# Fused sequence kernel, attention stage: which engine copies the first turned block and evicts q

## Chip, cores and metric

The kernel runs on one core of one Trainium2 chip. A core has a matrix engine (TensorE, PE in the profile, with PEld for its weight loads), a vector engine (VectorE, DVE), a scalar engine (ScalarE, ACT), a general one (GpSimd, POOL), a sync engine whose queue issues most DMAs here (SyncE, SP), and DMA engines. Each engine works through its own queue in order; semaphores tie them together. The metric is the device time of the whole program in microseconds (us), lower is better; the median over runs counts.

## The reference, cut to what matters

Four layers follow each other over 8 batches of 512 x 512 numbers: a grid step (finite differences of `f` with coefficient grids), an attention block with a feed-forward network, a mixture-of-experts feed-forward, and a low-rank gated response. The change is in the attention:

```python
q = (x @ Wq + bq).reshape(B, S, N_HEAD, HEAD_DIM).transpose(0, 2, 1, 3)
k = (x @ Wk + bk).reshape(B, S, N_HEAD, HEAD_DIM).transpose(0, 2, 1, 3)
v = (x @ Wv + bv).reshape(B, S, N_HEAD, HEAD_DIM).transpose(0, 2, 1, 3)
scores = jnp.einsum('bhqd,bhkd->bhqk', q / math.sqrt(HEAD_DIM), k)
scores = scores + attention_bias
scores = jnp.where(src_mask, -jnp.inf, scores.astype(jnp.float32))
probs = jax.nn.softmax(scores, axis=-1).astype(v.dtype)
ctx = jnp.einsum('bhqk,bhkd->bhqd', probs, v)
```

There are 16 heads of 32 features; everything is computed in 32-bit floats.

## The kernel before

**Stages.** `fused_kernel` runs a grid stage for batch 0, then `attention_stage` over all 8 batches, then `mlp_stage`. The attention stage also does the grid step of the next batches on the side: `grid_step` deals out the operations in the table `GRID`, mostly on VectorE (`gv`, line 697, and line 798), with a ReLU (line 804) and a small DMA issue behind it (line 806) on ScalarE, for each half of a batch's rows.

**Steps.** The main loop (from line 1137) goes over 128 units `(b, c, r)`: batch, group of four heads, quarter of the 512 query rows. A step of the loop has three units in hand. For the one of two steps ago TensorE multiplies probabilities with v (`values`, every second step). For the one of the step before, `turned` transposes the probabilities on TensorE (line 570, into tiles `tr` of PSUM) and copies them to SBUF (`pt`, lines 1052 and 1054). For the present one `softmax` adds the bias and takes the row's extreme on VectorE (line 1022, `mn`), and exponentiates on ScalarE (line 1027). The step ends with `scores` of the next unit. Between them, in `fill`, lie the projections: `q_block`, `k_block`, `v_block` and `o_block` (TensorE, line 567), the way of the next batch's x into transposed form (`x1_in`) and back (`x1_back`), and the loads of its mask (`load_mask`: a DMA, line 588, and a conversion on ScalarE, line 593). GpSimd adds the mask to the bias (line 998). In the texts below, step t of batch b is the pass of the loop in which the present unit is number t = 4c + r of that batch; it turns unit t - 1.

**What sets the order.** Nearly every instruction is pinned by `keep_in_program_order`, so each engine's queue is the order of the Python code. In `turned` the four heads of a unit come in two calls, u = 0 with heads 0 and 1, u = 1 with heads 2 and 3. There are two `tr` tiles, so the transposes of head 2 need head 0 copied out, those of head 3 need head 1. A rule (lines 1046 to 1054) says which engine copies: head 1 and head 3 always ScalarE, head 2 always VectorE, and head 0 by a list `early` of units, VectorE where it isn't in the list. The list is all of the first 8 units in batch 0, (1, 3, 4, 5, 7, 9, 15) in batches 1 to 6, and empty in batch 7.

**q.** `q_block` (line 634) multiplies into one PSUM tile of tag `m`, which the other projections and `add_bv` (the row `pb`) share, and VectorE writes it to SBUF with the bias added and scaled by 1/sqrt(32) (line 643). k's eviction (line 663) is on ScalarE.

**The bias of q** comes by a DMA (line 181) into `bqk[:, 0, :]`, 128 partitions of 4 numbers.

Of the kernel before, what the change touches and what calls it, by code (L numbers as in the profile page):

```python
# [15 lines left out]
AF = mybir.ActivationFunctionType  # L16
ALU = mybir.AluOpType
# [15 lines left out]
QSCALE = 1.0 / math.sqrt(HD)  # L33
# [6 lines left out]
def fused_kernel(ctx: ExitStack, tc: tile.TileContext, a: dict):  # L40
# [155 lines left out]
    def load_late():  # L196
# [3 lines left out]
    wl3 = const.tile([P, KC, RK], F32, name="wl3")  # L200
    x1d = [dram.tile([P, R, D], F32, name=f"x1d_{b}") for b in range(NB)]
    first = attention_stage(
        tc, a, small, dram, xp, xt, x_home, x1d, grid, ident, sc1, shift, io, wo8, w, (bqk, bvc, bo),
        g2, mhalf, load_w, load_late,
# [340 lines left out]
def attention_stage(  # L545
# [12 lines left out]
    nc = tc.nc  # L558
    with ExitStack() as ctx:
# [4 lines left out]
        pin = tc.keep_in_program_order  # L564
# [4 lines left out]
        def tp(out, src):  # L569
            pin(nc.tensor.transpose(out, src, ident))  # L570


        bqk, bvc, bo = rows
# [53 lines left out]
        def block(out, lhsT, rhs):  # L627

            def half(h):
                for k in (2 * h, 2 * h + 1):  # L630
                    mm(out, lhsT(k), rhs(k), k == 0, k == KC - 1)
            return half

        def q_block(b, c, tag="m"):
            pr = ps.tile([P, S], F32, name=f"pq_{b}_{c}", tag=tag)
            half = block(
                pr, lambda k: w["Wq"][:, k, c * P : (c + 1) * P], lambda k: x1s[b, k]
            )
            yield half(0)
            yield half(1)  # L640
            t = pp.tile([P, S], F32, name=f"qt_{b}_{c}", tag="qt")
            pin(
                nc.vector.tensor_scalar(
                    t.rearrange("f (r p) -> f r p", r=R), pr.rearrange("f (p r) -> f r p", r=R),
                    bqk[:, 0, c : c + 1], QSCALE, ALU.add, ALU.mult,
                )
            )
            qs[b, c] = t
# [266 lines left out]
        def halves(b):  # L915

            for g in (
                q_block(b, 1), k_block(b, 1), q_block(b, 2), k_block(b, 2), o_block(b - 1, 0),
                q_block(b, 3), k_block(b, 3), *(o_block(b - 1, r) for r in (1, 2, 3)),
            ):  # L920
                next(g)
                yield
                for _ in g:
                    pass
                yield

        def fill(b, t):
# [15 lines left out]
            if n == NB:  # L943
                if t == 0:
                    head["fill"] = halves(b)
                jobs.append(
                    next(head["fill"], None)
                    for _ in range({0: 2, 7: 2, 8: 2, 11: 2, 12: 2, 13: 0, 14: 2, 15: 0}.get(t, 1))
                )
            elif t in (0, 4, 8):  # L950
                jobs.append(q_block(b, t // 4 + 1))
            elif t in (1, 5, 9):
                turn = (lambda c: x1_in(n, c)) if t == 9 else None
                jobs.append(k_block(b, t // 4 + 1, turn=turn))
            elif t in (2, 3, 6, 7):
                if b:
                    jobs.append(o_block(b - 1, (2, 3, 6, 7).index(t)))
            elif t == 11:
                jobs.append(q_block(n, 0))
            elif t == 13:  # L960
                jobs.append(k_block(n, 0))
            else:
                jobs.append(v_block(n, (10, 12, 14, 15).index(t)))
# [15 lines left out]
        bias, ss, sums = {}, {}, {}  # L979
        pts, ctxs = {}, {}  # L980

        def load_bias(b, c, r):
            for u in range(2):
                hp = 2 * c + u
                bt = pp.tile([P, 2, S], F32, name=f"bt_{b}_{r}_{hp}", tag="bt", bufs=8)
                pin(
                    nc.sync.dma_start(
                        bt,
                        a["bias"][b, 2 * hp : 2 * hp + 2].rearrange("h (p r) k -> r p h k", r=R)[r],
                    )  # L990
                )
                bias[b, c, r, u] = bt
# [40 lines left out]
        def turned(b, c, r, u):  # L1033

            bt = bias.pop((b, c, r, u))
            for i in range(2):
                h = 2 * u + i
                if r % 2 == 0:
                    pts[b, c, r // 2, h] = pp.tile(
                        [P, KC, 2, P], F32, name=f"pt_{b}_{c}_{r}_{h}", tag=f"pt{h}", bufs=1  # L1040
                    )
                pt = pts[b, c, r // 2, h]
                tr = ps.tile([P, KC, P], F32, name=f"tr_{b}_{c}_{r}_{h}", tag="tr", bufs=2)
                for k in range(KC):
                    tp(tr[:, k, :], bt[:, i, k * P : (k + 1) * P])
                t = 4 * c + r
                if b == NB - 1:
                    early = ()
                else:
                    early = range(8) if b == 0 else (1, 3, 4, 5, 7, 9, 15)  # L1050
                if i == 0 and not (u == 0 and t in early):
                    pin(nc.vector.tensor_copy(pt[:, :, r % 2, :], tr))  # L1052
                else:
                    pin(nc.scalar.copy(pt[:, :, r % 2, :], tr))  # L1054
# [58 lines left out]
        mask_in(0, 0)  # L1113
        grid_loads(1, -2)
        load_bias(*units[0])
        load_w("Wv")
        grid_loads(1, -1)
        mask_in(0, 1)
        load_bias(*units[1])
        load_w("Wo")  # L1120
        for c in range(KC):
# [7 lines left out]
        drain(k_block(0, 0, "ctx"))  # L1129
        mask_out(0, 1)  # L1130
        load_bias(*units[2])
        mask_in(0, 2)
        mask_in(0, 3)
# [3 lines left out]
        for i in range(n + 2):  # L1137
# [11 lines left out]
            for u in range(2):  # L1149
                if old:  # L1150
                    turned(*old, u)
                if now:
                    softmax(*now, u)
                next(jobs, None)
# [910 lines left out]
```

## Time and profile before

| what | us |
|---|---|
| median of 3 runs | 2697.31 (2696.57 to 2699.41) |
| the profiled execution, its time | 2701.51 |
| its span, first to last instruction | 2699.7 |
| attention stage in it | some 59 to 1095 |
| TensorE busy in the span | 2649.8 |
| VectorE busy | 1930.8 |
| ScalarE busy | 960.9 |
| GpSimd busy | 1480.9 |
| copies of turned blocks on ScalarE (line 1054) | 306, 172.6 busy |
| copies of turned blocks on VectorE (line 1052) | 206, 141.9 busy |
| evictions of q on VectorE (line 643) | 32, 0.71 each |

The page of a profile lists busy time of each engine, the span in 40 slices, the DMA queues, the chain of waits that ended last, and groups of like instructions. Rows of a timeline read: start in us, duration, engine, line, operation, tile written and tiles read, shape, count of merged instructions, and in brackets how long the engine had been idle before and what released it. A "q" behind the engine's name is its sequencer: it issues or waits while the engine itself is idle. A matrix product of four blocks shows as eight matmul rows.

### The profile page before, as it was taken

To read this page: it belongs to the slowest core of one execution; us is meant where nothing else is said; L and a number is where in the kernel's file an instruction comes from. 1 tells how busy PE (TensorE), PEld (TensorE's weight loads), DVE (VectorE), ACT (ScalarE), POOL (GpSimd) and SP (SyncE) were. 2 spreads that over 40 slices of the span, in tenths; PEclk is the share of its full clock that TensorE was granted. 3 is DMA by queue.
4 is the path that set the end of the run, shared out by engine and by line. 5 is a ranking of instruction groups with operands and counts; after the bars stand their busy time and mean duration, and the time that the engine had idled before them with its cause. 6 is when DMAs were issued, how large, how long until landed. Compare 5 with 4: busy or idle time off the path is not lost.

```text
span 2699.7 us, 39350 instructions
## 1 busy us (share of the span) xinstructions
PE 2649.8 (98%) x14182; PEld 1959.2 (73%) x14182; DVE 1930.8 (72%) x3538; ACT 960.9 (36%) x1997; POOL 1480.9 (55%) x1090
## 2 busy tenths in 40 slices
PE   7999999999999999999999999999999999999998
PEld 4455555555555555788888888888888888888887
DVE  7888898989898756576666656656555766666665
ACT  2566666666666666212212211210111211211221
POOL 3455565655555655366566465555555555555543
PEclk9999999999999999999999999999999999999999
DMA  8765757666676554644453543455335346345421
GB/s 308 253 217 194 247 193 242 212 215 231 230 240 211 167 170 157 194 144 117 138 156 98 162 146 100 148 156 154 120 116 184 127 150 194 124 145 198 121 100 42
DMA packets 241760, 460.31 MB, mean 171 GB/s; under 512 B 33848, under 2 KB 77440, under 8 KB 232478
## 3 DMA queue, kind: packets, MB, share of 16 engines
q1 hardware_dynamic: 237754, 447.04, 49.2%
q0 software_dynamic: 3360, 10.68, 3.0%
q8 instruction: 113, 1.85, 0.3%
q14 instruction: 81, 0.66, 0.1%
q10 hardware_dynamic: 452, 0.07, 0.0%
HBM read 398.43 MB, written 55.09 MB: 168 GB/s over the span
## 4 chain that ended last, share of the span: by engine, by line
PE 90%; DVE 4%; DMA 3%; ACT 1%; SPq 1%; issue 1%; POOL 0%; ACTq 0%; DVEq 0%; POOLq 0%
PE u L1208 29%; PE y L1208 28%; PE tr L570 8%; PE s L567 5%; PE o L567 4%; PE ctx L567 4%; PE pq L567 4%; PE pv L567 3%; PE pk L567 3%; DMA mu<-in_mask 2%; DVE bt L1022 1%; PE l L251 1%; DMA rd<-rt 1%; DVE x L697 1%; DVE pt L1052 1%
## 5 line engine op out<-in xcount | busy, mean ns | idle before, releaser
L998 POOL TENSOR_TENSOR bt<-bt,mk 128x1024 f32<-128x1024 f32 x256 | 543.7, 2148 | 72.6 <-DMA bt<-in_bias 67.2
L1208 PE MATMUL y<-wo,act 128*128 128x256 f32 x2560 | 566.3, 380 | 0.0
L1208 PEld LDWEIGHTS y<-wo,act 128*128 128x128 f32 x2560 | 484.5, 190 | 71.6 <-issue 6.7
L1027 ACT ACTIVATE bt<-bt,mn 128x512 f32<-128x512 f32 x512 | 365.7, 716 | 87.7 <-DVE mn L1022 86.4
L570 PEld LDWEIGHTS tr<-ident,bt 128*128 128x128 f32 x2048 | 229.4, 142 | 159.9 <-issue 97.5
L1022 DVE CUSTOM_DVE_ANT_0 bt<-s,bt 128x512 f32<-128x512 f32 x512 | 330.8, 684 | 2.2 <-PE s L567 2.0
L1208 PE MATMUL u<-bt,wi 128*128 128x256 f32 x1440 | 330.5, 379 | 0.0
L1214 DVE TENSOR_TENSOR act<-u,u 128x512 f32<-128x512 f32 x256 | 173.2, 684 | 200.6 <-PE u L1208 132.5
L1208 PEld LDWEIGHTS u<-bt,wi 128*128 128x128 f32 x1440 | 273.5, 190 | 37.2
L570 PE MATMUL tr<-ident,bt 128*128 128x128 f32 x2048 | 278.2, 278 | 15.1 <-ACT pt L1054 12.9
L1208 PE MATMUL u<-tb,ws 128*128 128x256 f32 x1024 | 242.2, 379 | 0.0
L1054 ACT COPY pt<-tr 128x512 f32<-128x512 f32 x306 | 172.6, 581 | 179.0 <-PE tr L570 176.3
L1208 PE MATMUL y<-t,s 128*128 128x256 f32 x1024 | 227.8, 380 | 0.0
L1217 POOL TENSOR_TENSOR t<-wo,t 128x512 f32<-128x512 f32 x64 | 107.3, 1699 | 203.1 <-PE y L1208 203.1
L1052 DVE COPY pt<-tr 128x512 f32<-128x512 f32 x206 | 141.9, 689 | 106.2 <-PE tr L570 100.2
L1208 PEld LDWEIGHTS u<-tb,ws 128*128 128x128 f32 x1024 | 194.3, 190 | 26.6 <-DVE tb L1214 0.2
L1208 PEld LDWEIGHTS y<-t,s 128*128 128x128 f32 x1024 | 194.0, 190 | 26.1
L1572 ACT ACTIVATE act<-act,b 128x512 f32<-128x512 f32 x128 | 82.9, 712 | 292.8 <-DVE act L1214 292.8
L1572 ACT ACTIVATE act<-act,bi 128x512 f32<-128x512 f32 x128 | 83.8, 712 | 282.6 <-DVE act L1214 282.6
L567 PE MATMUL s<-kt,qt 32*128 32x512 f32 x1024 | 175.9, 640 | 2.0 <-DVE mn L1022 1.0
L1591 ACT COPY u<-u 128x512 f32<-128x512 f32 x64 | 36.4, 568 | 393.3 <-PE u L1208 278.2
L1214 DVE TENSOR_TENSOR x<-y,x 128x512 f32<-128x512 f32 (+1 forms) x97 | 64.7, 680 | 154.0 <-PE y L1208 103.7
(323 smaller groups left out, 4144.5 us busy)
## 6 DMA issues: line engine op xcount, KB each, us to landing
bt<-in_bias SPq DMA_DIRECT2D x256, 512.0 KB
wo<-in_W SPq DMA_DIRECT2D x32, 1024.0 KB
wi<-in_Wi SPq DMA_DIRECT2D x32, 1024.0 KB
wo<-in_Wo_e SPq DMA_DIRECT2D x32, 1024.0 KB
wi<-in_W SPq DMA_DIRECT2D x28, 1024.0 KB
td<-tt SPq DMA_DIRECT2D x22, 1024.0 KB
bt<-td SPq DMA_DIRECT2D x176, 128.0 KB
gq<-coef_q SPq DMA_DIRECT2D x21, 512.0 KB
```

The lines of the kernel that those rows point to most:

```text
L567: pin(nc.tensor.matmul(out, lhsT=lhsT, rhs=rhs, start=start, stop=stop))
L570: pin(nc.tensor.transpose(out, src, ident))
L998: nc.gpsimd.tensor_tensor(bt, bt, mask[b, r][:, None, :].to_broadcast([P, 2, S]), ALU.add)
L1022: nc.vector.tensor_tensor_reduce(bt[:, i, :], ss[h], bt[:, i, :], -1.0, 3.0e38, ALU.add, ALU.min, mn)
L1027: nc.scalar.activation(bt[:, i, :], bt[:, i, :], AF.Exp, bias=mn, scale=-1.0, accum_out=sums[b, c][:, h, r : r + 1],)
L1052: pin(nc.vector.tensor_copy(pt[:, :, r % 2, :], tr))
L1054: pin(nc.scalar.copy(pt[:, :, r % 2, :], tr))
L1208: pin(nc.tensor.matmul(out, lhsT=lhsT, rhs=rhs, start=start, stop=stop))
L1214: pin(nc.vector.tensor_tensor(out, x, y, op))
L1217: pin(nc.gpsimd.tensor_tensor(out, x, y, op))
L1572: nc.scalar.activation(acts[g][:, k, :], acts[g][:, k, :], func, bias=bi[:, j : j + 1])
L1591: pin(nc.scalar.copy(u1, p[0]))
```

## The change

It does three things. The list `early` becomes all 16 units in batches 0 to 6, so that head 0's copy is on ScalarE in every step of these batches; batch 7 is left as it was. q's eviction becomes an activation with the function Identity on ScalarE, with the bias and the scale as its operands. As the activation scales first and adds the bias afterwards, the bias is multiplied by the scale once, on GpSimd, before the loop.

```diff
@@ q_block @@
             pin(
-                nc.vector.tensor_scalar(
+                nc.scalar.activation(
                     t.rearrange("f (r p) -> f r p", r=R), pr.rearrange("f (p r) -> f r p", r=R),
-                    bqk[:, 0, c : c + 1], QSCALE, ALU.add, ALU.mult,
+                    AF.Identity, bias=bqk[:, 0, c : c + 1], scale=QSCALE,
                 )
             )
@@ attention_stage, ahead of load_bias @@
         pts, ctxs = {}, {}
 
+        pin(nc.gpsimd.tensor_scalar_mul(bqk[:, 0, :], bqk[:, 0, :], QSCALE))
+
@@ turned @@
                 if b == NB - 1:
                     early = ()
                 else:
-                    early = range(8) if b == 0 else (1, 3, 4, 5, 7, 9, 15)
+                    early = range(16)
                 if i == 0 and not (u == 0 and t in early):
```

## The prediction

> **What bounds it now.** I read the page first: busy shares and the chain of waits. TensorE is busy 98% of the span and 90% of the chain is TensorE; VectorE, from which work is taken, has 4% of it.
>
> ```profile
> PE 90%; DVE 4%; DMA 3%; ACT 1%; SPq 1%; issue 1%; POOL 0%; ACTq 0%; DVEq 0%; POOLq 0%
> ```
>
> Then the timeline of the attention stage (59 to 1095 us), one step at a time. I call a step by its number t in its batch (0 to 15); it turns the probabilities of unit t-1. Here are the score matmuls that end three steps running of batch 5:
>
> ```profile
> 718.09 1.14 PE L567 MATMUL s<-kt,qt 32*128 32x512 f32 x8
> 724.50 1.14 PE L567 MATMUL s<-kt,qt 32*128 32x512 f32 x8
> 732.77 1.14 PE L567 MATMUL s<-kt,qt 32*128 32x512 f32 x8
> ```
>
> The distances, 6.41 and 8.27 us, come back to the hundredth in the like steps (t = 0, 1, 3, 4, 5, 15) of all batches from 2 to 6: TensorE runs without a gap there, and relief elsewhere is worth nothing. So only steps longer than this floor can gain, and the question is whether some step now falls off it.
>
> **The naive sum.** 62 copies leave VectorE (8 of batch 0, 9 in each of batches 1 to 6; 0.689 us each) and 32 evictions of q (0.724): 65.9 us. ScalarE gains 62 x 0.581 and 32 x some 0.70: 58 us, at 588 busy of 925 us between 170 and 1095. Neither is the bound, so both sums are for orientation only. What counts is the queue order of ScalarE: two accumulators ("tr", two buffers) hold the turned blocks of heads 0 and 1, and the transposes of head 2 wait until head 0 is copied out, about 2.19 us after head 0's are done. Before, head 0 left by VectorE in these steps; now it stands in ScalarE's queue, ahead of head 1, behind whatever ScalarE waits for.
>
> **Steps 7 of batches 1 to 6: slower.** ScalarE has the grid's ReLU (L804) and a DMA issue (L806) ahead of the copies:
>
> ```profile
> 773.49 0.69 DVE L1052 COPY pt<-tr 128x512 f32<-128x512 f32 x1
> 773.61 1.06 ACT L804 ACTIVATE x<-x 128x1024 f32<-128x1024 f32 x1 [3.03 <-DVE x L798]
> 774.69 0.22 ACTq L806 DMA_DIRECT2D x<-xed  x1
> 774.96 0.59 ACT L1054 COPY pt<-tr 128x512 f32<-128x512 f32 x1 [0.29 <-ACT x L804]
> 775.18 1.08 PE L570 MATMUL tr<-ident,bt 128*128 128x128 f32 x8
> ```
>
> The 773.49 copy moves to 774.96 and ends at 775.55; the transposes of head 2 start at about 775.59 instead of 775.18. Head 1's copy follows 0.5 later, just in time for head 3. Plus 0.4 us, six times: **+2.4**. In step 1 the ReLU is done 0.2 us before head 1's copy could start (728.30 to 728.56), so nothing is lost there.
>
> **Steps 13: slower.** At the end of step 12 ScalarE is given a mask conversion (L593) whose DMA has not landed; the copies queue behind it. Batch 1:
>
> ```profile
> 317.74 0.69 DVE L1052 COPY pt<-tr 128x512 f32<-128x512 f32 x1 [0.57 <-PE tr L570]
> 319.70 0.60 PE L570 MATMUL tr<-ident,bt 128*128 128x128 f32 x4
> 321.21 0.63 ACT L593 ACTIVATE mk<-mu 128x512 bf16<-128x512 uint8 x1 [6.30 <-DMA mu<-in_mask]
> 321.75 0.57 ACT L1054 COPY pt<-tr 128x512 f32<-128x512 f32 x1
> 322.37 1.11 PE L570 MATMUL tr<-ident,bt 128*128 128x128 f32 x4 [2.07 <-ACT pt L1054]
> ```
>
> Here head 2 was turned during the wait (319.70) and only head 3 had to wait. Afterwards head 0's copy takes the 321.75 place, head 1's comes 0.5 later, and head 2 is turned after the wait as well: four transposes, some 0.5 us, more behind it. Queued behind the copies are this step's four exponentials and k's eviction; they slip by the same 0.5 us as TensorE, whose step 14 reads them, so nobody else comes to wait. All seven batches 0 to 6 wait in step 13: 7 x 0.48 = **+3.4**. Step 14 waits in batches 0 and 2 to 5 for the next mask; its landing is set by the DMA queue, not by TensorE, so the 0.5 of step 13 is swallowed by that wait and charged once more by the same mechanism: no further sum.
>
> **Steps 11: faster.** VectorE copies head 0 late, behind grid work (556.39 to 557.08 in batch 3), and TensorE waits 0.50, 0.19, 0.33 and 0.25 us in batches 1, 2, 3 and 5. ScalarE is idle 2.67 us before its copy there. **-1.3**. The score stalls of steps 2, 6 and 10 stay: VectorE's run that causes them begins after its head-2 copy had waited for TensorE (0.6 to 1.1 us idle), or with a wait for a DMA, and nothing in that run is moved.
>
> **Batch 0, step 1: faster.** The q of step 0 stood behind eight grid operations on VectorE, and the next matmul into the same accumulator waited for it:
>
> ```profile
> 92.72 0.74 DVE L643 TENSOR_SCALAR qt<-pq,bqk 128x512 f32<-128x512 f32 x1
> 93.52 5.40 PE L567 MATMUL pb<-Wo,bvr 128*128 128x512 f32 x8 [1.96 <-DVE qt L643]
> 96.32 1.07 ACT L1054 COPY pt<-tr 128x512 f32<-128x512 f32 x2 [0.31 <-ACT x L804]
> ```
>
> ScalarE is free from 87.7, and q's matmul ends at 89.4: pb starts at 91.4, at full clock (3.44), and ends at 94.85 instead of 98.8. Late next are ScalarE's copies: VectorE's L798 comes 0.67 earlier, so the ReLU, and the copies start at 95.65; the transposes go on at 96.3 instead of 98.76. **-2.4**, if nothing downstream is tied to a fixed time; GpSimd waits for no bias DMA between 88 and 216, and the other loads are issued behind TensorE's progress.
>
> **At nothing.** The other q evictions: a ScalarE row of this kind costs between 0.669 (k's, L663) and 0.768 (L612, permuted); I take 0.70, as its read is permuted like L612's but its scale is a constant. It stands behind the last exponential and is over before the next copies; the tightest is step 12 (686.56 + 0.70, next copy possible 687.8). Uncovered, 7 x up to 0.7 = 5 us. GpSimd's multiply of 128x4: 0.23 us by its L432 rows, in front of 9.86 us of idle time; bq landed long before. It delays no mask add. Copies in steps 3, 9, 12, 15: ScalarE idle before them.
>
> **The clock.** The section on HAM oscillation in the Trainium skill's page "TensorE: Matmul & The Clock Gate" asks for no idle gap over about 3.4 us. The longest gap that I expect is 2.6 us, so by the rule the change costs no clock. The rows say that less is enough (stretch, length, then TensorE's busy time; the granted clock is the third number from the end):
>
> ```profile
> 318.91:322.32 3.41, 1.39 (x7) 0.62 (x5) 2.65 (x9) 1.10 (x3) 2.77 (x2) 1.00 0.63 156
> 322.32:325.73 3.41, 3.36 (x7) 1.92 (x8) 0.00 (x0) 3.31 (x9) 0.00 (x0) 0.50 0.93 334
> 946.96:950.37 3.41, 1.88 (x11) 1.24 (x10) 1.91 (x5) 2.40 (x6) 0.00 (x0) 1.00 0.82 250
> ```
>
> After a stretch with 1.39 us busy the clock was halved for 3.41 us (pk 3.11 instead of 1.88, tr 1.11 instead of 0.66: some 1.7 us lost); after 1.88 busy it was not. Without head 2's transposes in between, the idle gap of batch 6 grows from 1.53 to about 2.1, of batch 1 from 2.07 to 2.6. By the rows one window more or less in batch 0, 1 or 6: -1.7 to +5.1. I take +0.6, a third of a window.
>
> **Sum.** 2.4 + 3.4 - 1.3 - 2.4 + 0.6 = +2.7 us. The profiled execution took 2701.5 (span 2699.7 and 1.8 around it), 4.2 over the median of 2697.3; batch 1's mask wait, with its half-speed window, is the outlier in it (its step 13 is 12.67 us, the others' 9.2 to 10.5). On the median: **2700.0**.
>
> **Rivals.**
> (A) As summed, 55%: 2700.0, own range 2695 to 2702.7.
> (B) The clock: from the third extra half-speed window on, in the gaps of steps 13 and 14 that head 2 no longer splits (decided below some 1.5 to 1.9 us busy in a window): 2699.4 + 3 x 1.7 = 2704.5. For it: batch 1's row. Against: the other gaps are 1.0 to 1.6 us. 24%.
> (C) Batch 0's gain is lost at its own mask wait (step 14 waits for a DMA that took 8.1 us to land): 2700.0 + 2.4 = 2702.4, on the border. 12%.
> (D) Faster: the mask lands 0.9 to 2.8 us earlier relative to step 13, so its toll is gone; -2.4 - 1.3 + 2.4 = -1.3, and with batch 1's half-speed window and wait gone and pb's whole 4.1 us kept, down to 2691. Against: the mask's issue follows the round trip of the row sums, which the change doesn't touch. 8%.
> That VectorE bounds and 65.9 us come back (2631) is excluded by the floors: 1%.
>
> **Chances.** 0.2% (5.4 us) is about what a measurement of this kernel can tell from no change. Slower by more: B, half of C, the tail of A: 0.35. Faster: most of D: 0.08. Between: 0.57. The range reaches into B and D: 2693.5 to 2707.5.
>
> **What would show it.** Step 7 of batches 1 to 6 at about 8.7 instead of 8.31; transposes of head 2 in step 13 behind the mask conversion; step 11 at 8.74 throughout; pb in batch 0 unstalled and at full clock; floors of 6.41 and 8.27 unchanged. I am wrong if floors move, if q's eviction holds up the first copies, or if several more half-speed windows appear.

## The result, and the profile after

The changed kernel takes 2707.72 us (median of 12 runs, 2703.39 to 2712.27); the kernel before took 2698.36 beside it (2695.29 to 2701.9). The ratio is 1.0035, with a 95% interval of 1.0026 to 1.0044: some 9.4 us slower, where 2.7 were forecast and the range ended at 2707.5. The profiled execution took 2706.44.

The page of the changed kernel, its busy shares, its chain of waits and the two groups of copies (columns of a group: shape and count, then busy us, mean ns | idle before it and what ended most of that):

```profile
span 2704.7 us, 39416 instructions
...
PE 2646.0 (98%) x14182; PEld 1955.1 (72%) x14182; DVE 1887.5 (70%) x3444; ACT 1007.2 (37%) x2091; POOL 1476.1 (55%) x1091
...
PE 84%; DVE 4%; POOL 3%; DMA 3%; issue 3%; SPq 1%; ACT 1%; POOLq 0%; ACTq 0%; DVEq 0%
...
L1056 ACT COPY pt<-tr 128x512 f32<-128x512 f32 x368 | 203.5, 584 | 170.5 <-PE tr L570 168.4
L1054 DVE COPY pt<-tr 128x512 f32<-128x512 f32 x144 | 99.5, 691 | 173.5 <-PE tr L570 172.5
```

62 copies went from VectorE to ScalarE as counted, and VectorE lost 43 us of busy time, where 65.9 had been forecast to leave it: part of the rest is one of its small operations, L819, whose 14 instructions took 16.5 us instead of 5.5. None of the relief shows in the span. What is new is in the chain: GpSimd had 0% of it and now has 3%, TensorE 84% instead of 90%. No GpSimd work of any weight was added, so something now waits for GpSimd that did not. (Lines behind 980 are two higher than before: L1054 and L1056 are the copies of VectorE and ScalarE, L1000 is the mask add.)

**Step by step.** I compared the lengths of the 127 steps from one end of a step's scores to the next. Since a single profile can be an odd one, each kernel was profiled a second time (below); the two right-hand columns are after minus before, in us.

| where | forecast | first profiles | second profiles |
|---|---|---|---|
| step 7, batches 1 to 6 | +2.4 | +2.96 | +2.99 |
| step 8, batches 1 to 6 | 0 | **+7.61** | **+7.47** |
| steps 10, batches 0 to 6 | 0 | -3.0 | -2.73 |
| steps 11 | -1.3 | -1.4 | -3.05 |
| steps 13 and 14 | +3.4 | +2.78 | +2.77 |
| batch 0, step 1 | -2.4 | -2.53 | **-0.46** |
| batch 0, steps 2 to 7 | in "the clock", +0.6 | +1.63 | +2.79 |
| all else | 0 | -3.12 | -0.68 |
| span | +2.7 | +4.93 | +9.11 |

Step 8 is the largest row and was not in the forecast at all: 7.70 us instead of 6.41, in each of the six batches.

**What happens there.** First the kernel before, batch 5, timeline (start, duration, engine, line, tiles, and in brackets the idle time before and what ended it); step 8 begins at 778.98:

```profile
774.89 8.42 POOL L998 TENSOR_TENSOR bt<-bt,mk 128x1024 f32<-128x1024 f32 x4
...
778.62 0.51 DVE L819 SCALAR_TENSOR_TENSOR gsh<-gmv,grs 128x2 f32<-128x2 f32 x1
...
779.17 1.52 ACT L823 ACTIVATE x<-x,gsh,grs 128x512 f32<-128x512 f32 x2 [0.32 <-DVE gsh L819]
...
780.59 1.05 ACT L1054 COPY pt<-tr 128x512 f32<-128x512 f32 x2
...
781.62 1.04 PE L570 MATMUL tr<-ident,bt 128*128 128x128 f32 x8
```

Then the same place in the changed kernel; step 8 begins at 784.83:

```profile
778.96 1.06 ACT L804 ACTIVATE x<-x 128x1024 f32<-128x1024 f32 x1 [3.04 <-DVE x L798]
...
780.24 8.40 POOL L1000 TENSOR_TENSOR bt<-bt,mk 128x1024 f32<-128x1024 f32 x4
780.31 1.07 ACT L1056 COPY pt<-tr 128x512 f32<-128x512 f32 x2 [0.29 <-ACT x L804]
...
781.04 1.06 PE L570 MATMUL tr<-ident,bt 128*128 128x128 f32 x8 [0.35 <-ACT pt L1056]
...
783.86 0.69 DVE L689 TENSOR_TENSOR x<-o,x 128x512 f32<-128x512 f32 x1 [0.25 <-PE o L567]
...
784.47 2.10 DVE L819 SCALAR_TENSOR_TENSOR gsh<-gmv,grs 128x2 f32<-128x2 f32 x1
...
786.61 1.52 ACT L823 ACTIVATE x<-x,gsh,grs 128x512 f32<-128x512 f32 x2 [1.92 <-DVE gsh L819]
...
788.03 1.05 ACT L1056 COPY pt<-tr 128x512 f32<-128x512 f32 x2
...
788.74 1.06 PE L570 MATMUL tr<-ident,bt 128*128 128x128 f32 x8 [1.10 <-POOL bt L1000]
```

Read it from the middle. L819 is the shift of a norm, which VectorE computes for the grid step; `gsh` is its result. Head 0's copy stands behind the ReLU, and the transposes of head 2 start at 781.04, with the wait that was forecast. VectorE's L689 waits for TensorE's o and slips with it, and L819 behind it. L819 computes 128 x 2 numbers. GpSimd's mask adds do not slip: they begin 0.22 us behind the end of the ReLU in both kernels (774.67 and 774.89, 780.02 and 780.24). Four of them run beside L819, 8.40 / 4 = 2.10 us each, so one ends at 780.24 + 4.20 = 784.44 and the next at 786.54. Before, L819 began 3.73 us after the first add had begun, had 0.48 us to the end of the second add, and took 0.51. Now it begins 4.23 us after, 0.03 past that boundary, and takes 2.10: it ends with the third add. In all six batches it takes 0.51 to 0.53 before and 2.10 or 2.11 after. Slipping by 0.5, it now takes 2.10 where it took 0.51. ScalarE's norm (L823) needs its result and stands ahead of the copies of step 8, so both copies are late (788.03) and TensorE stops. The last row's bracket names GpSimd, which is how GpSimd came into the chain; the instruction that had really been late is the copy, ended at about 788.6.

### The profile page after: what moved, and what is told of

It reads as the page before. It is cut to its first block, busy times and chain, and to the rows that moved or that the text cites. A ratio compares the mean times of both kernels' runs of the same rounds, so it can differ in the third digit from the quotient of the medians.

```text
span 2704.7 us, 39416 instructions
## 1 busy us (share of the span) xinstructions
PE 2646.0 (98%) x14182; PEld 1955.1 (72%) x14182; DVE 1887.5 (70%) x3444; ACT 1007.2 (37%) x2091; POOL 1476.1 (55%) x1091
## 4 chain that ended last, share of the span: by engine, by line
PE 84%; DVE 4%; POOL 3%; DMA 3%; issue 3%; SPq 1%; ACT 1%; POOLq 0%; ACTq 0%; DVEq 0%
PE u L1210 29%; PE y L1210 28%; PE tr L570 6%; PE s L567 4%; PE ctx L567 3%; POOL bt L1000 3%; PE pq L567 3%; PE pv L567 3%; PE o L567 2%; PE pk L567 2%; DMA mu<-in_mask 2%; DVE bt L1024 1%; DVE x L697 1%; PE l L251 1%; DVE pt L1054 1%
## 5 line engine op out<-in xcount | busy, mean ns | idle before, releaser
L1000 POOL TENSOR_TENSOR bt<-bt,mk 128x1024 f32<-128x1024 f32 x256 | 540.5, 2136 | 70.4 <-DMA bt<-in_bias 52.0
L1056 ACT COPY pt<-tr 128x512 f32<-128x512 f32 x368 | 203.5, 584 | 170.5 <-PE tr L570 168.4
L1054 DVE COPY pt<-tr 128x512 f32<-128x512 f32 x144 | 99.5, 691 | 173.5 <-PE tr L570 172.5
```

Of the source, the lines that this page charges most:

```text
L1000: nc.gpsimd.tensor_tensor(bt, bt, mask[b, r][:, None, :].to_broadcast([P, 2, S]), ALU.add)
```

## The experiments

Each ran beside the kernel before. Times are medians, ratios are against the kernel before with the 95% interval. Where a list of units is shown, it is written more simply than in the run and holds the same units.

**Unit 6 back on VectorE.** The changed kernel, with head 0 of step 7 copied by VectorE again in batches 1 to 6:

```diff
-                    early = range(16)
+                    early = [v for v in range(16) if b == 0 or v != 6]
```

> The changed kernel with one unit put back: head 0 of unit 6 in batches 1 to 6 is copied by VectorE again. Theory (a chain): in step 7 that copy stands behind the grid's ReLU on ScalarE and makes the step 0.5 us longer; by this slip a small VectorE operation (L819, the shift of the norm) just misses the end of a GpSimd instruction and waits for the whole next one, ScalarE's norm waits for it, and the copies of step 8 wait behind the norm: 1.28 us more. Then step 7 is back at 8.31, step 8 at 6.41, 10.6 us in six batches, of which some 2.7 come back as waits in step 10, where the row sums' DMA lands at its own time: 2699 to 2701 us. Rival (the mask waits and half-speed windows carry the excess): step 7's own 0.5 alone goes, 2704 to 2706.

Measured: 2699.04 us, ratio 1.0004 (0.9995 to 1.0012). Steps 7 and 8 are back at 8.31 and 6.41. So one copy in six batches carries most of the 9.4 us (8.7 between the two medians, 7.7 if each is taken against the kernel before that ran beside it), and step 8 depends on step 7's copy. Of the 2.7 us that I expected to come back as waits in step 10, 0.8 did.

**Unit 6 alone.** The kernel before with nothing but that copy moved:

```diff
-                    early = range(8) if b == 0 else (1, 3, 4, 5, 7, 9, 15)
+                    early = range(8) if b == 0 else (1, 3, 4, 5, 6, 7, 9, 15)
```

> The kernel before with the copy of head 0 in step 7 (unit 6) of batches 1 to 6 moved to ScalarE, and nothing else. My theory: step 7 is 0.49 us longer and step 8 is 1.2 to 1.3 us longer through the wait of VectorE's L819 for GpSimd, six times: +10 us, 2705 to 2708 us (ratio 1.003 to 1.004). Rival: the wait of step 8 needs the other moves as well (VectorE's order without q and the other copies); then only step 7's 0.49 x 6 = 3 us are paid, 2700 to 2701 us, and step 8 stays at 6.41.

Measured: 2704.41 us, ratio 1.0028 (1.0019 to 1.0038); step 7 at 8.80 and step 8 at 7.70, as the theory said, so no other move is needed. The time is just under its band. Steps 7 and 8 add 10.6 us, and steps 10 and 11, where a DMA is waited for, give back 3.8 against the first profile of before and 5.2 against the second. Steps 13 and 14 are 1.9 and 1.6 shorter, but most or all of that lies in batch 1's step 13, which varies from one execution to the next.

**L819's product on GpSimd.** All of the change kept, but the shift is computed by GpSimd behind the power that it needs, so VectorE has no instruction there:

```diff
@@ behind the power on GpSimd @@
+                sh = small.tile([P, 2], F32, name=f"gsh_{n}_{j}", tag="gsh", bufs=2)
+                pin(nc.gpsimd.tensor_tensor(sh, mv[:, :, 0], rs, ALU.mult))
+                pin(nc.gpsimd.tensor_scalar(sh, sh, -1.0, None, ALU.mult))
+                gs[n, "sh"] = sh
@@ line 817 @@
-                sh = small.tile([P, 2], F32, name=f"gsh_{n}_{p}", tag="gsh", bufs=2)
-                pin(
-                    nc.vector.scalar_tensor_tensor(sh, mv[:, :, 0], -1.0, rs, ALU.mult, ALU.mult)
-                )
+                sh = gs[n, "sh"]
```

> The changed kernel with the shift of the norm computed by two small GpSimd operations right behind the power, instead of by VectorE in L819; nothing else. Theory (L819 waits for the end of a GpSimd instruction, and ScalarE's copies of step 8 wait for it): step 7 stays at 8.80, step 8 returns to 6.41, 7.6 us, of which up to 2.7 come back in step 10: 2700 to 2703 us. Rival (step 8 is late because ScalarE itself has too much in its queue): step 8 stays near 7.70, 2706 to 2709.

Measured: 2699.95 us, ratio 1.001 (1.0001 to 1.0019), just under its band. Its timeline, batch 5, step 8 from 777.43:

```profile
774.93 6.33 POOL L1001 TENSOR_TENSOR bt<-bt,mk 128x1024 f32<-128x1024 f32 x3
...
777.18 1.52 ACT L820 ACTIVATE x<-x,gsh,grs 128x512 f32<-128x512 f32 x2
...
778.60 1.06 ACT L1057 COPY pt<-tr 128x512 f32<-128x512 f32 x2
...
780.08 1.04 PE L570 MATMUL tr<-ident,bt 128*128 128x128 f32 x8
```

The norm follows ScalarE's last exponential at once, with no bracket, and the copies are 1.17 us behind the beginning of step 8 instead of 3.20. Step 8 is at its floor of 6.41 in batches 1 to 6 while step 7 still has its 0.49 to 0.52. This separates the two: the copy's place behind the ReLU makes step 7's loss, L819 beside GpSimd makes step 8's.

**Units 12 and 13 back on VectorE** (steps 13 and 14, the mask conversions), the rest of the change kept:

```diff
-                    early = range(16)
+                    early = [v for v in range(16) if v not in (12, 13)]
```

> The changed kernel with head 0 of units 12 and 13 in batches 0 to 6 copied by VectorE again, so that head 0 isn't queued behind the mask conversions. Theory (the chain through step 8 carries most): steps 7 and 8 stay at 8.80 and 7.70, steps 13 and 14 lose 0.5 us a batch, 2703 to 2705 us. Rival (mask waits and half-speed windows carry the excess): 2698 to 2701, and fewer half-speed windows than in the changed kernel.

Measured: 2702.9 us, ratio 1.002 (1.0013 to 1.0026), just under its band. That is 4.8 less than the changed kernel by the medians and 3.9 less if each is taken against the kernel before beside it, where 3.4 had been forecast for these copies; steps 7 and 8 stay at 8.80 and 7.70. As its rival had it, there are fewer half-clock stretches than in the changed kernel: none is left in steps 13 and 14 (see "The clock" below).

**q alone.** The kernel before with q's eviction on ScalarE and the bias scaled beforehand; `early` as before.

```diff
-                nc.vector.tensor_scalar(
+                nc.scalar.activation(
...
-                    bqk[:, 0, c : c + 1], QSCALE, ALU.add, ALU.mult,
+                    AF.Identity, bias=bqk[:, 0, c : c + 1], scale=QSCALE,
...
+        pin(nc.gpsimd.tensor_scalar_mul(bqk[:, 0, :], bqk[:, 0, :], QSCALE))
```

> The kernel before with q's eviction alone on ScalarE and its bias scaled beforehand; the list of copies as before. Theory: pb in batch 0 no longer waits, 2.5 us less, nothing else moves: 2695 to 2697 us. Rival (q's eviction gets in the way of the first copies of the next step): steps 1, 5, 9 and 12 leave their floors of 8.27, 8.27, 10.38 and 6.87, 2699 us or more.

Measured: 2695.32 us, ratio 0.9988 (0.998 to 0.9996). Steps 1, 5, 9 and 12 of batches 1 to 6 keep their floors: the eviction, 0.69 us on ScalarE, holds up nobody. A small gain; its profile is shorter in steps 10 and 11 (108.2 us, where the kernel before has 110.4 and 111.8) and in batch 0's step 1.

**The copies alone.** The kernel before with the list alone changed to `range(16)`:

```diff
-                    early = range(8) if b == 0 else (1, 3, 4, 5, 7, 9, 15)
+                    early = range(16)
```

> The kernel before with only the first turned copies of every step moved to ScalarE; q's eviction stays on VectorE, its bias unscaled. My theory: the copies alone carry the loss, and the q move gains on its own: step 7 of batches 1 to 6 at 8.80 and step 8 at 7.70 us as in the changed kernel, batch 0's step 1 without its 2.5 us gain, so 2708 to 2712 us (ratio 1.004 to 1.0055). Rival: the q evictions on ScalarE share in the loss by standing ahead of copies; then this kernel is faster than the changed one, 2700 to 2704 us, and step 8 or 13 shorter than there.

Measured: 2706.32 us, ratio 1.0036 (1.0023 to 1.0049), inside neither band. Steps 7 and 8 are as in the changed kernel, so the copies carry the loss. But batch 0's step 1 was 3.34 us shorter than in the first profile of before, although nothing of the code up to there differs. The gain that I had booked for q was there without q's move.

**Both kernels once more.**

> The kernel before, unchanged, for a second profiled execution of it. Open: in the profiles of kernels whose code is the same up to step 7 (the one with only unit 6 moved, the one with the copies only), batch 0's step 1 had its old length once and was 3.34 us shorter once, and step 10 of batches 2 to 5 was 0.3 to 0.9 us shorter in nearly all. Theory: these two differences are between executions of the same code (which instruction of GpSimd VectorE meets, and where the clock windows fall), not the change's; then step 10 of batches 3 to 5 is here 0.5 to 0.9 us shorter than in the first profile of before, and step 1 of batch 0 either like it or 2.5 to 3.9 us shorter. Rival: the change causes them; then every step of this profile outside steps 13 and 14 is within 0.1 us of the first. Time 2694 to 2702 us.

> The changed kernel, unchanged, for a second profiled execution of it. Theory: steps 7 and 8 of batches 1 to 6 are again at 8.80 and 7.6 to 7.7 us (set by the order of the queues, so the same each time), while the half-clock windows and the waits of steps 13 and 14 fall differently. Rival: steps 7 and 8 vary from one execution to the next by more than 0.3 us. Time 2703 to 2712 us.

Measured: 2697.68 us (ratio 0.9998, 0.9987 to 1.001) and 2706.22 (1.0033, 1.0022 to 1.0044). Steps 7 and 8 of the changed kernel are the same to 0.03 us as in its first profile. The kernel before, unchanged, has its step 1 of batch 0 2.48 us shorter than the first time. Its timeline now:

```profile
92.38 0.74 DVE L643 TENSOR_SCALAR qt<-pq,bqk 128x512 f32<-128x512 f32 x1
...
93.18 3.70 PE L567 MATMUL pb<-Wo,bvr 128*128 128x512 f32 x8 [1.18 <-DVE qt L643]
```

and the same in the changed kernel:

```profile
89.17 0.69 ACT L643 ACTIVATE qt<-pq,bqk 128x512 f32<-128x512 f32 x1 [1.80 <-PE pq L567]
...
91.07 3.60 PE L567 MATMUL pb<-Wo,bvr 128*128 128x512 f32 x8
```

The first profile had 1.96 us of wait and 5.40 us of matmuls at half clock; this one has 1.18 and 3.70 at full clock. The change does take the wait away, but the end of the step is set by VectorE's grid work and the ReLU behind it, and the step is only 0.05 (first profile of after) to 0.46 us (second) shorter than in this execution. Over all profiles, batch 0's step 1 takes 10.0 to 11.6 us in the eight with q on ScalarE, and 10.60, 11.46, 13.94 and 13.94 in the four with q on VectorE. So the move may well take away the long case, but how much it brings on average is not shown.

As to step 10, the second profile of before differs from the first by -0.66 to +0.54 a batch, where I expected -0.5 to -0.9, and its steps 11 are longer; the two together are 110.4 us in the first, 111.8 in the second, 106.0 in both profiles of after. This gain belongs to the change, and my theory for this part fell.

**What step 10 waits for.** The second profile of before, batch 3, step 10 from 543.63 (SPq rows: the sync engine issues):

```profile
532.69 0.32 SPq L1081 DMA_DIRECT2D rd<-rt  x1
...
541.23 1.75 SPq L1086 DMA_DIRECT2D rbs<-rd  x4
...
545.03 0.69 DVE L1098 TENSOR_TENSOR ct<-ctx,rbs 128x512 f32<-128x512 f32 x1 [1.22 <-DMA rbs<-rd]
```

The changed kernel, step 10 from 549.82:

```profile
538.77 0.32 SPq L1083 DMA_DIRECT2D rd<-rt  x1
...
544.53 1.75 SPq L1088 DMA_DIRECT2D rbs<-rd  x4
...
549.92 0.69 DVE L1100 TENSOR_TENSOR ct<-ctx,rbs 128x512 f32<-128x512 f32 x1
```

The reciprocals of the row sums go out to memory (rd, 16 KB) and come back (rbs). VectorE waited 1.22 us for them, and step 10's `mn`, then the scores, and in step 11 more grid work were late behind it. From one issue to the next it took 8.54 us before and 5.76 after; from rd to the beginning of step 10 it is 11 us in both. The rows of busy time in the last stretch ahead of the rbs issue (stretch, length, busy time of the engines, clock, busy share of the DMA engines, GB/s) show the DMA engines emptier. First profile of before, where rd to rbs took 8.48, then after:

```profile
538.10:542.60 4.50, 4.50 (x24) 2.70 (x22) 3.85 (x11) 3.76 (x9) 3.41 (x2) 1.00 0.94 373
```

```profile
542.80:547.00 4.20, 4.20 (x24) 2.66 (x22) 2.41 (x6) 3.40 (x9) 2.73 (x2) 1.00 0.63 241
```

The grid's loads start at 523.00 before and at 525.87 after, so 11.1 and 12.9 us ahead of rd: the slip of steps 7 and 8, 1.8 us, is time in which the loads drain. With unit 6 alone the time was as short (5.52). With unit 6 back, no slip and VectorE relieved, it took 7.41, and in batch 3 the wait was gone as well, so the slip seems one way to lose this wait and less work on VectorE another. But the second profile of after has 7.22 there and no wait either. That the earlier loads made the time short is read from these rows, not tested by itself, and what sets the wait of step 10 stays open in part.

**Mask loads earlier.** The changed kernel, with the mask's DMAs (`mask_in`) one or two steps earlier; the conversions (`mask_out`) stay.

```diff
+                if t in (10, 11, 13, 14):
+                    jobs.append(mask_in(n, (10, 11, 13, 14).index(t)) for _ in range(1))
                 if t >= 12:
-                    jobs.append(load_mask(n, t - 12) for _ in range(1))
+                    jobs.append(mask_out(n, t - 12) for _ in range(1))
```

> The changed kernel with the DMAs of the next mask issued one or two steps earlier (at steps 10, 11, 13 and 14; the conversions stay where they are). My theory: the landing of the mask sets the waits of steps 13 and 14, whichever engine copies; with it early the conversion waits for nothing, steps 13 and 14 of batches 0 to 6 come down by 1 to 3 us a batch, and fewer half-clock windows appear there: 2690 to 2698 us (ratio 0.997 to 1.0003 against the kernel before). Rival: the wait moves to another load (the bias or the weights queue behind the mask) or ScalarE's queue itself is too long there: within 3 us of the changed kernel, 2704 to 2710 us.

Measured: 2689.46 us, ratio 0.9967 (0.9954 to 0.998), some 18 us under the changed kernel, slightly better than expected. Batch 5, step 13, in the changed kernel:

```profile
829.43 0.63 ACT L593 ACTIVATE mk<-mu 128x512 bf16<-128x512 uint8 x1 [4.76 <-DMA mu<-in_mask]
...
829.96 1.06 ACT L1056 COPY pt<-tr 128x512 f32<-128x512 f32 x2
...
830.68 1.07 PE L570 MATMUL tr<-ident,bt 128*128 128x128 f32 x8 [1.07 <-ACT pt L1056]
```

and with early masks:

```profile
807.76 0.63 ACT L593 ACTIVATE mk<-mu 128x512 bf16<-128x512 uint8 x1
...
810.73 1.07 ACT L1058 COPY pt<-tr 128x512 f32<-128x512 f32 x2 [2.35 <-PE tr L570]
...
812.63 1.04 PE L570 MATMUL tr<-ident,bt 128*128 128x128 f32 x8
```

The conversion waits for nothing, is over before the transposes whose copies stand behind it, and the bracket of the copies names TensorE. Steps 13 are 8.74 and steps 14 6.87 in all seven batches, where the changed kernel has 9.6 to 13.2 and 6.87 to 13.0. The landing of the mask set those waits, in the kernel before too.

**The parts that gained.** q on ScalarE, unit 10 added to the list of before, early masks. The list alone is shown; the rest is as above.

```diff
-                    early = range(8) if b == 0 else (1, 3, 4, 5, 7, 9, 15)
+                    early = range(8) if b == 0 else (1, 3, 4, 5, 7, 9, 10, 15)
```

> The parts that gained, together: q on ScalarE with the scaled bias, of the copies only step 11's moved in addition to those of the kernel before, and the mask's DMAs issued earlier. My theory: the gains add up: -2 us (q), -1.3 us (step 11), -10 to -17 us (mask waits of steps 13 and 14): 2677 to 2684 us (ratio 0.9925 to 0.995). Rival: the mask's early DMAs only move the wait elsewhere: 2693 to 2696 us.

Measured: 2680.49 us (2679.6 to 2681.98), ratio 0.9936 (0.9923 to 0.9949): 17.5 us faster than the kernel before, 27 than the changed one. Against the second profile of before, steps 13 and 14 bring 15.0 us. Its chain has GpSimd at nothing:

```profile
PE 94%; DVE 3%; DMA 1%; ACT 1%; issue 0%; SPq 0%; ACTq 0%; POOL 0%; DVEq 0%; POOLq 0%
```

## Why the prediction was wrong

**The step that failed** is "Plus 0.4 us, six times: +2.4". The mechanism in step 7 was right, and its size nearly (+0.49 each, +2.96). But the slip was priced by its own length and taken to end there. I followed what stood behind the copies on ScalarE and in TensorE, not what slips with TensorE on VectorE: L689 waits for o, and behind it L819, whose length depends on where in GpSimd's instruction it begins. 0.5 us late at that place cost 1.29 more in step 8, +7.5 in six batches, which the prediction had put at nothing. The row that could have told me was in the trace of before: L819 takes 0.51 us at 778.62 (shown above), but 0.15 where no mask add runs:

```profile
534.63 0.15 DVE L819 SCALAR_TENSOR_TENSOR gsh<-gmv,grs 128x2 f32<-128x2 f32 x1
```

So most of the 0.51 is a wait, not work.

The Trainium skill states this. Its page "SBUF — State Buffer", section "SBUF: two separate sides", says that VectorE and GpSimd share a pair of ports, which a VectorE operation with two SBUF inputs and a GpSimd operation that reads SBUF hold for a whole instruction, the other blocking until then. Both inputs of L819 (gmv and grs) are in SBUF. This case agrees: in both profiles of both kernels L819 takes 0.12 to 0.15 us where no mask add runs, and beside one up to 2.11, ending each time within 0.03 us of the end of a mask add. It was the rule that spoke against this change, and I weighed only the one on the clock.

**Batch 0, step 1, -2.4**: met to 0.1 us in the first profiles, by luck. I worked it out against an execution whose wait and half-clock matmuls another execution of the same code had less of. Beside the second profile the change brings 0.05 to 0.46; its average gain stays open (see the twelve profiles' figures above).

**"The score stalls of steps 2, 6 and 10 stay"**: wrong for step 10; steps 10 and 11 gain 4.4 to 5.8. **Steps 11, -1.3**: the steps came to 8.74 as forecast. The reason given is enough by what the last kernel shows (it moves unit 10's copy, has no slip, and its steps 11 are at 8.74 in all seven batches while step 10 still waits), but the slip does the same in batches 1 to 6 with unit 6 alone, where unit 10's copy stays on VectorE. What steps 10 and 11 gave back hid part of the first error.

**Steps 13, +3.4**: right in mechanism. Batches 0 and 2 to 5 rose by 0.28 to 0.79 each, where 0.48 was forecast; batch 6 fell by 0.8, and batch 1 moved by -2.35 in one pair of profiles and +2.19 in the other. One pair says little here. Five of the kept profiles have the copies of these steps on ScalarE behind late masks (the changed kernel twice, unit 6 back, L819's product on GpSimd, the copies alone) and five on VectorE (the kernel before twice, unit 6 alone, units 12 and 13 back, q alone): steps 13 and 14 of batches 0 to 6 sum to 127.1 to 131.1 us in the former and to 122.3 to 124.6 in the latter, 5.1 apart in the mean. **q's eviction, GpSimd's multiply, steps 3, 9, 12, 15 at nothing**: right. **The floors** held, outside step 8.

**The clock, +0.6, and rival B**: the mechanism is there, the size of B is not. The stretches at half clock between 50 and 1105 us sum to 20.5 and 13.7 us in the two profiles of before and to 20.5 and 20.5 in those of after; at half a stretch lost, that is 0 to 3.4 us. Most fall early, and differently each time: in batch 0's steps 2 to 7 the change of place made part of the +1.6 to +2.8. But in the mask gaps of steps 13 and 14 the ten profiles differ as the copies do: stretches of 3.41 us are there 2, 1, 2, 1 and 1 times in the five with the copies on ScalarE, and 1, 0, 0, 0 and 0 times in the five with them on VectorE. So the gaps that head 2 no longer splits do cost clock, about one stretch an execution, not the three and more of B; it is part of the 5.1 us. With the masks early there are none. The prediction put the border at some 1.5 to 1.9 us of TensorE work in a stretch, where its rows say 1.39 to 1.88; these (columns as there) narrow it:

```profile
944.34:947.75 3.41, 1.41 (x5) 0.37 (x4) 0.00 (x0) 1.32 (x3) 0.00 (x0) 1.00 0.56 146
947.75:951.16 3.41, 3.41 (x11) 2.37 (x12) 1.91 (x5) 3.19 (x9) 1.91 (x1) 0.50 0.99 375
```

```profile
456.78:460.19 3.41, 1.58 (x10) 1.31 (x11) 0.91 (x2) 2.83 (x7) 2.41 (x2) 1.00 0.76 279
460.19:463.60 3.41, 3.41 (x31) 1.62 (x33) 2.69 (x6) 3.07 (x9) 0.00 (x0) 1.00 0.66 204
```

The first pair is from the kernel with L819's product on GpSimd, batch 6, the second from the copies alone, batch 2. Cut all twelve profiles between 150 and 1060 us into such stretches, in step with their half-clock ones: the seven times that the clock went down, TensorE had been busy 0.16 to 1.41 us in the stretch before, and with 1.58 or more at full clock it never went down. Before 150 us busy time alone doesn't tell: in batch 0's steps 6 and 7 the clock went down behind stretches with 2.1 to 3.3 us busy as well.

**Rival C** is not settled. In the first profiles batch 0's step 14 is 4.1 us longer, with two half-clock stretches in it, more than its step 1 gained; in the second it is 0.8 longer.

With the second profiles: 3.0 + 7.5 - 5.8 + 2.8 - 0.5 + 2.8 - 0.7 = 9.1 us, beside 9.4 by the medians.

## What to carry to other kernels

When a step slips, list on every engine the instructions that wait for the slipped work, and look at each for a neighbour whose instruction it must outwait; a slip of half a microsecond can cost most of the length of the neighbour's instruction (here 1.29 of 2.10 us). A short instruction that now and then takes several times its usual time marks such a place; moving it off the path brought step 8 back to its floor here. Don't book a gain from one execution's wait before you know that other executions have it; and look for a wait for a DMA that stands in every period: here issuing the mask earlier brought more (15.0 us in steps 13 and 14) than any relief of VectorE.

## What the hardware showed that I had not expected

A VectorE operation on 128 x 2 numbers took 0.15 us alone and up to 2.10 beside GpSimd's mask adds of 2.10 each. Copies from PSUM by VectorE beside the same adds keep 0.68 to 0.69. The clock's stretches at half speed, 3.41 us or multiples of it, came at other places in each execution of the same program, and for the kernel before to 13.7 us in one and 20.5 in the other; behind a mask gap they came only after 1.41 us or less of TensorE work in the 3.41 us before. And from the issue of a 16 KB write to that of the reads behind it, it took 8.5 us in both profiles of before and 5.8 or 7.2 in those of after (batch 3); why is not shown.
